# Copying the displaced signs of a binary shift convolution by GpSimd alone, with three sign buffers and transfers by channel tile

## The chip, the cores and the metric

The kernel runs on one core of one Trainium2 chip. The metric is the device time of one execution in microseconds (us). Of the kernel before there are three runs: 2382.28, 2384.86 and 2385.98 us, so the median is 2384.86 us. A separate profiled execution took 2382.86 us, and the span that its trace shows is 2381.1 us.

## The reference

The input `x` has one image of 384 channels and 192 x 192 pixels in float32. Two layers are applied, each as a residual on a group norm over 32 groups of 12 channels (`_gn`).

```
x = x + _L0_conv_ref(_gn(x), ...)   # layer 0: 1x1 conv to q,k,v; 2x2 max pool; 3x3 depthwise conv;
                                    # channel attention, four top-k softmaxes; gelu; repeat 2x2; 1x1 conv
x = x + _L1_conv_ref(_gn(x), weight, bias)
```

Layer 1 is the part that the change touches:

```
def _L1_conv_ref(x, weight, bias):
    K = 7
    xb, wb = sign(x), sign(weight)
    dx = (jnp.arange(C) + K // 2) % K - K // 2
    xp = jnp.pad(xb, ((0, 0), (0, 0), (0, 0), (P, P)))
    idx = jnp.arange(W)[None, :] + dx[:, None] + P
    shifted = jnp.take_along_axis(xp, idx[None, :, None, :], axis=3)
    return jnp.einsum('bchw,oc->bohw', shifted, wb) + bias[None, :, None, None]
```

Each channel's signs are shifted along the row by its own `dx`, one of -3 to 3 (about 55 channels have each value), with zeros moved in at the row's ends, and then a 384 x 384 matrix of signs is applied at every pixel. Because only the sign of the group norm is used, the mean of the group is needed and the variance is not.

## The kernel before

The 384 channels lie as three channel tiles (`CT` = 3) of 128 partitions. The 192 rows are cut into 24 units (`NU`) of 8 rows, so one tile `xt` holds three channel tiles of 1536 float32 values on each partition, 2304 KB in all. The first 2030 us of the span are the statistics of layer 0, its q and k (lines 311 to 366), the softmaxes, and v with the attention. They leave the attention's output in six `chunk` tiles, each of four units. The change leaves their instructions as they are.

The last stage, under `with end:` (line 592), does the rest of both layers for one unit after another. It begins when the group means of layer 1 (`nmean1`, line 587) are known. For each unit there are three steps, whose order is written out by hand:

- `summed(i)` ends layer 0 for the i-th unit of the list `order`. For each of three output channel tiles TensorE runs six matmuls on the chunk into `yps` (L488), and VectorE adds the result to `xt` in two instructions (L497). There are two `yps` buffers. When the last unit of a chunk is done, the chunk's buffer takes an x tile.
- `signed(i)` makes the signs. ScalarE writes them as fp8 into `signs`, in six instructions of 64 partitions (L667): three channel tiles, two halves of partitions. The channels are sorted by shift on the host (`shift_halves`), so that nearly all of a half have one shift, and the half is written displaced by it. In each half, 9 or 10 channels have shift 0 and fill it up. These are written with the wrong displacement, and `centred` brings them back: the rows are copied to `rest`, by small DMAs for channel tiles 0 and 1 (L644) and by GpSimd in 16-bit words for tile 2 (L646), and then GpSimd copies them from `rest` to the right place in `signs` (L655). That copy works byte by byte in tiles 0 and 2, whose place is odd, and in 16-bit words in tile 1.
- `finished(i)` applies the sign matrix: 36 fp8 matmuls into `l1ps` (L687, three buffers of two banks), and six VectorE instructions that add the product and the bias to `xt` in place (L695).

Two sign buffers alternate. The loop runs `summed(i + 2)`, `finished(i)`, `signed(i + 2)`. So the signs of unit i + 2 are written into the buffer that `finished(i)` has just read, while TensorE goes on with `summed(i + 3)` and `finished(i + 1)`.

The data moves in whole units. `stored(i - 2)` is issued on ScalarE's DMA queue from within `signed(i)` (L703). Loads are on SyncE's queue (L171), which also carries the small copies of L644. A load into the buffer of an earlier unit waits on that queue for that unit's store. At the stage's start three units are there (`FIRST`, which are units 19 and 18, and unit 23), and a fourth buffer, `more`, takes a load. The other buffers come free with the chunks.

Of the kernel before, what the change touches and what calls it, by code (L numbers as in the profile page):

```python
# [10 lines left out]
F32 = mybir.dt.float32  # L11
F8 = mybir.dt.float8e4
U16 = mybir.dt.uint16
BF16 = mybir.dt.bfloat16
AF = mybir.ActivationFunctionType
ALU = mybir.AluOpType
# [3 lines left out]
P = 128  # L20
C = 384
CT = C // P
# [8 lines left out]
UR = 8  # L31
NU = H // UR
# [6 lines left out]
PITCH = W + 4  # L39
LEAD = 4  # L40
SLEN = UR * PITCH
HALF = P // 2

STEP = 1584
SAT = [16 + t * STEP + t - SHIFT // 2 for t in range(CT)]
SALL = SAT[-1] + SLEN + PITCH + 9
REST = 32
NREST = [[9, 9], [9, 9], [10, 9]]
ABLK = 512
NAB = NPX // ABLK  # L50
UC = 4
# [8 lines left out]
FIRST = (NU - UC - 1, NU - UC - 2)  # L60
# [17 lines left out]
def shift_halves():  # L78


    dx = lambda c: (c % SHIFT + SHIFT // 2) % SHIFT - SHIFT // 2
    of = {d: [c for c in range(C) if dx(c) == d] for d in range(-(SHIFT // 2), SHIFT // 2 + 1)}
    shift = [[t - SHIFT // 2, t + 1] for t in range(CT)]
    at = np.zeros((P, CT), int)
    for t in range(CT):
        for h, d in enumerate(shift[t]):
            n = NREST[t][h]
            at[h * HALF : (h + 1) * HALF, t] = of[d][:REST] + of[0][:n] + of[d][REST:]
            of[0] = of[0][n:]
    assert sorted(at.flat) == list(range(C))  # L90
    return at, shift


XCH, HSHIFT = shift_halves()


def pair_rows():
# [40 lines left out]
def conv_preact_kernel(ctx: ExitStack, tc: tile.TileContext, a: dict, out: bass.AP):  # L138
    nc = tc.nc
    xv = a["x"].rearrange("u t p n -> u p t n")  # L140
    ov = out.rearrange("u t p n -> u p t n")
# [4 lines left out]
    big = ctx.enter_context(tc.tile_pool(name="big", bufs=NBIG))  # L146
# [5 lines left out]
    parts = {name: small[:, i:j] for name, i, j in SMALL}  # L152
# [7 lines left out]
    nmean1 = const.tile([P, CT], F32, name="nmean1")  # L160
# [6 lines left out]
    def unit(u, pool=big, parts=1):  # L167
        xt = pool.tile([P, CT, UPX], F32, name="xt", tag="big")
        n = CT // parts
        for t in range(0, CT, n):  # L170
            nc.sync.dma_start(xt[:, t : t + n], xv[u][:, t : t + n])  # L171
        return xt
# [36 lines left out]
    kept = {}  # L209
    with tc.tile_pool(name="p1", bufs=1, side="right") as p1, tc.tile_pool(name="p1ps", bufs=2, space=PSUM) as psp:  # L210
# [5 lines left out]
        for i in range(NU):  # L216
            u = NU - 1 - i
            xt = unit(u, parts=CT if u in (0, NU - 1) else 1)
# [13 lines left out]
            else:  # L232
                b, k = divmod(seen, BATCH)
                seen += 1
                for t in range(CT):
                    for j in range(UPX // 512):
                        at = (k * (UPX // 512) + j) * 6
# [14 lines left out]
        more = p1.tile([P, CT, 2], F32, name="more")  # L252
# [26 lines left out]
        shift = p1.tile([NG, 1], F32, name="shift")  # L279
# [59 lines left out]
    with tc.tile_pool(name="p2w", bufs=1, side="right") as wp, tc.tile_pool(  # L339
        name="p2t", bufs=2, side="right"  # L340
    ) as tp, tc.tile_pool(name="p2qkv", bufs=3, space=PSUM) as pqkv, tc.tile_pool(
        name="p2tr", bufs=2, space=PSUM
# [4 lines left out]
        for u in range(NU):  # L347
            xt = kept.pop(u) if u in kept else unit(u)
            lo, hi = rows(u)
            n = hi - lo + 1  # L350
# [149 lines left out]
    with ExitStack() as vs:  # L500
# [39 lines left out]
        for u in range(NU):  # L540
            xt = unit(u)
# [9 lines left out]
            for m in range(CT):  # L551
                parts = []
                for c in range(first // CR, last // CR + 1):
                    r0, r1 = max(first, c * CR), min(last, c * CR + CR - 1)
# [37 lines left out]
    with end:  # L592
        more, sp = opened("p5x1", 1), opened("p5s", 1)
        pyp, psp = opened("p5py", 2, space=PSUM), opened("p5ps", 3, space=PSUM)
        signs = [sp.tile([P, SALL], F8, name=f"signs{i}") for i in range(2)]
        rest = sp.tile([P, CT, SLEN], F8, name="rest")

        def half_rows(sg, t, h):

            at = SAT[t] - HSHIFT[t][h]  # L600
            return sg[h * HALF : (h + 1) * HALF, at : at + SLEN].rearrange("p (r w) -> p r w", w=PITCH)[:, :, :W]


        assert SALL % 4 == LEAD % 4 == PITCH % 4 == 0
        for sg in signs:
            words = sg.bitcast(F32)
            for t in range(CT):
                for h in range(2):
                    at, odd = divmod(SAT[t] - HSHIFT[t][h] - LEAD, 4)
                    assert not odd  # L610
                    lead = words[h * HALF : (h + 1) * HALF, at : at + (UR + 1) * PITCH // 4]
                    nc.gpsimd.memset(lead.rearrange("p (r w) -> p r w", w=PITCH // 4)[:, :, : LEAD // 4], 0.0)
        order = [u for c in reversed(range(NCH)) for u in reversed(range(c * UC, (c + 1) * UC))]
        order = [*FIRST, *(u for u in order if u not in FIRST)]
        left = [UC] * NCH
        free = [more]
        todo = [u for u in order if u not in kept]
        home = {u: big for u in kept} | {FIRST[0]: early}

        def loads():  # L620
            while free and todo:
                u = todo.pop(0)
                home[u] = free.pop(0)
                kept[u] = unit(u, home[u])

        def summed(i):

            u = order[i]
            if i >= len(FIRST):
                for m in range(CT):  # L630
                    projected(pyp.tile([P, PPX], F32, name="yps"), u, m)
            left[u // UC] -= 1
            if not left[u // UC]:
                free.append(big)
                loads()

        def centred(sg, t):

            for h in range(2):
                p = slice(h * HALF + REST, h * HALF + REST + NREST[t][h])  # L640
                at = SAT[t] - HSHIFT[t][h]
                src, to = sg[p, at : at + SLEN], rest[p, t]
                if t < CT - 1:
                    nc.sync.dma_start(to.bitcast(F32), src.bitcast(F32))  # L644
                else:
                    nc.gpsimd.tensor_copy(to.bitcast(U16), src.bitcast(U16))  # L646
            for h in range(2):
                p = slice(h * HALF + REST, h * HALF + REST + NREST[t][h])
                src, to = (
                    v.rearrange("p (r w) -> p r w", w=PITCH)[:, :, :W]  # L650
                    for v in (rest[p, t], sg[p, SAT[t] : SAT[t] + SLEN])
                )
                if SAT[t] % 2 == 0:
                    src, to = src.bitcast(U16), to.bitcast(U16)
                nc.gpsimd.tensor_copy(to, src)  # L655

        def signed(i):


            if i > 2:  # L660
                free.append(home[order[i - 3]])
                loads()
            xt, sg = kept[order[i]], signs[i % 2]
            for m in range(CT):
                for h in range(2):
                    p = slice(h * HALF, (h + 1) * HALF)
                    nc.scalar.activation(  # L667
                        half_rows(sg, m, h),
                        xt[p, m, :].rearrange("p (r w) -> p r w", w=W),
                        AF.Sign,  # L670
                        bias=nmean1[p, m : m + 1],
                        saturate=False,
                    )
                if m == 0 and i > 1:
                    stored(i - 2)
                centred(sg, m)

        def finished(i):

            xt, sg = kept[order[i]], signs[i % 2]  # L680
            for m in range(CT):
                for r0 in range(0, UR, 4):
                    ps = psp.tile([P, 2, 512], F32, name="l1ps")
                    for j in range(2):
                        for t in range(CT):
                            at = SAT[t] + (r0 + 2 * j) * PITCH
                            nc.tensor.matmul(  # L687
                                ps[:, j, : 2 * W],
                                wb[:, t, m * P : (m + 1) * P],
                                sg[:, at : at + 2 * PITCH].rearrange("p (r w) -> p r w", w=PITCH)[:, :, :W],  # L690
                                start=(t == 0),
                                stop=(t == CT - 1),
                            )
                    blk = xt[:, m, r0 * W : (r0 + 4) * W].rearrange("p (j n) -> p j n", j=2)
                    nc.vector.scalar_tensor_tensor(  # L695
                        blk, ps[:, :, : 2 * W], bl1[:, m : m + 1], blk, ALU.add, ALU.add
                    )
                if i >= NU - 2:
                    nc.scalar.dma_start(ov[order[i], :, m], xt[:, m])

        def stored(i):
            u = order[i]
            nc.scalar.dma_start(ov[u], kept.pop(u))  # L703

        with tc.manual_schedule():
            loads()
            for i in range(2):
                summed(i)
                signed(i)
            for i in range(NU):  # L710
                if i + 2 < NU:
                    summed(i + 2)
                finished(i)
                if i + 2 < NU:
                    signed(i + 2)


# [70 lines left out]
```

## Time and profile before

| what | value |
|---|---|
| median of three runs | 2384.86 us |
| span of the profile | 2381.1 us |
| busy, whole span | TensorE 91%, VectorE 77%, ScalarE 37%, GpSimd 10% |
| last stage | from 2030.6 us (the group means) to 2381.1 us |
| moved in the last stage | 21 loads and 24 stores of 2304 KB |

The share of TensorE says little of the last stage. The page's rows of tenths, in 40 slices of 59.5 us, show the last six at TensorE 7, 8, 9, 8, 8 and 7 tenths where all before from the third on are at 9, and GpSimd is at work in these alone. In a group's row the number after the bar is the busy time in us and the mean of one instruction in ns; after the second bar stands how long the engine sat idle just before these instructions, and what it waited for.

### The profile page before, as it was taken

Reading aid. Unit: us, or ns where it says so; the run is one execution under the profiler, and the core shown is the slowest. Engines: PE = TensorE matmul, PEld = TensorE weight load, DVE = VectorE, ACT = ScalarE, POOL = GpSimd, SP = SyncE. Lnnn points to the kernel's source line nnn. Section 1 sums busy time; section 2 is a strip of 40 time slices with the busy share of each in tenths; the row PEclk is TensorE's granted clock in tenths of the full one; section 3 lists DMA queues with packets and bytes.
Section 4 is the critical chain, followed back from the end, with each engine's and each line's share of the span. In section 5 each row is a group of like instructions: output and inputs, shape, how many; then the busy total and the mean of one; then the engine's idle time right before and its main releaser. Section 6 shows DMA issues by size and latency. Waiting matters only on the chain.

```text
span 2381.1 us, 19521 instructions
## 1 busy us (share of the span) xinstructions
PE 2166.2 (91%) x6573; PEld 1032.4 (43%) x6573; DVE 1826.7 (77%) x3113; ACT 878.2 (37%) x1564; POOL 227.5 (10%) x248
## 2 busy tenths in 40 slices
PE   1049999999999999999999999999999999789887
PEld 0024444454444454444444444444444444445444
DVE  4667777777777777777777789986878788678776
ACT  5532223322222332222322232244332323666665
POOL 0000000000000000000000000000000000646676
PEclk7569999999999999999999999999999999899998
DMA  9961111111111211110111022041212122499975
GB/s 398 418 248 40 40 40 46 74 40 40 40 40 40 80 40 40 40 40 0 60 60 40 1 88 101 1 166 73 80 45 115 40 94 90 179 369 364 372 293 209
DMA packets 48948, 272.90 MB, mean 115 GB/s; under 512 B 2896, under 2 KB 5072, under 8 KB 48848
## 3 DMA queue, kind: packets, MB, share of 16 engines
q1 hardware_dynamic: 37392, 211.34, 23.0%
q10 hardware_dynamic: 11456, 60.33, 6.3%
q8 instruction: 51, 0.84, 0.1%
q14 instruction: 49, 0.40, 0.1%
HBM read 213.68 MB, written 56.62 MB: 114 GB/s over the span
## 4 chain that ended last, share of the span: by engine, by line
PE 46%; DVE 33%; DMA 9%; ACT 8%; POOL 2%; issue 2%; SPq 0%; POOLq 0%; DVEq 0%; ACTq 0%
PE qkv L311 33%; DVE dw L334 18%; DVE pooled L318 9%; DMA xt<-in_x_dram 6%; PE l1ps L687 4%; DVE chunk L334 4%; DMA rest<-signs 3%; ACT pooled L325 3%; ACT dw L332 3%; PE gram L366 3%; PE yps L488 2%; PE ops L528 2%; PE tr L362 2%; DVE xt L497 2%; ACT sq L355 2%
## 5 line engine op out<-in xcount | busy, mean ns | idle before, releaser
L311 PE MATMUL qkv<-xt,wq 128*128 128x512 f32 x3888 | 1700.8, 593 | 0.3 <-DVE small L284 0.3
L311 PEld LDWEIGHTS qkv<-xt,wq 128*128 128x128 f32 x3888 | 726.4, 190 | 862.7 <-issue 797.4
L334 DVE SCALAR_TENSOR_TENSOR dw<-pooled,small,dw 128x384 f32<-128x384 f32 (+2 forms) x1152 | 709.3, 616 | 251.3 <-ACT dw L332 226.8
L318 DVE TENSOR_REDUCE pooled<-qkv 128x128 f32<-128x512 f32 x648 | 443.1, 685 | 79.2 <-PE qkv L311 72.9
L334 DVE SCALAR_TENSOR_TENSOR chunk<-pooled,small,chunk 128x384 f32<-128x384 f32 (+3 forms) x696 | 370.4, 546 | 73.5 <-ACT chunk L332 56.0
L336 ACT COPY pooled<-pooled 128x196 f32<-128x196 f32 x207 | 73.7, 356 | 743.2 <-DVE dw L334 520.4
L667 ACT ACTIVATE signs<-xt,nmean 64x1536 fp8e4<-64x1536 f32 x144 | 226.5, 1573 | 108.8 <-POOL signs L655 64.3
L325 ACT ACTIVATE pooled<-pooled,small 128x384 f32<-128x384 f32 x216 | 133.2, 617 | 332.3 <-DVE pooled L318 332.3
L687 PE MATMUL l1ps<-signs,wb 128*128 128x384 fp8e4 x864 | 163.2, 346 | 42.4 <-POOL signs L655 39.5
L655 POOL COPY signs<-rest 9x1536 fp8e4<-9x1536 fp8e4 (+1 forms) x144 | 180.5, 1254 | 133.2 <-DMA rest<-signs 127.0
L695 DVE SCALAR_TENSOR_TENSOR xt<-l1ps,small,xt 128x768 f32<-128x768 f32 x144 | 137.6, 1010 | 52.0 <-issue 23.1
L497 DVE SCALAR_TENSOR_TENSOR xt<-yps,small,xt 128x768 f32<-128x768 f32 x132 | 127.9, 1013 | 30.2 <-PE yps L488 24.3
L488 PE MATMUL yps<-chunk,wpr 128*128 128x384 f32 x396 | 138.4, 495 | 9.1 <-DVE xt L497 9.1
L687 PEld LDWEIGHTS <-wb 128*128 128x128 fp8e4 x864 | 88.1, 102 | 119.8 <-issue 64.3
L292 POOL MEMSET pooled<- 128x196 f32 x9 | 2.4, 267 | 1403.1 <-PE tr L362 1244.8
L355 ACT ACTIVATE sq<-dw 128x384 f32<-128x384 f32 (+2 forms) x144 | 75.3, 523 | 158.2 <-DVE dw L334 158.2
L238 DVE BATCH_NORM_STATS2 stats<-xt 128x6 f32<-128x512 f32 x144 | 87.2, 675 | 59.3 <-DMA xt<-in_x_dram 59.3
L188 PE MATMUL gsps<-sums,small 128*32 128x2 f32 x6 | 0.5, 197 | 127.0 <-DVE sums L259 127.0
L332 ACT ACTIVATE dw<-pooled,small 128x384 f32<-128x384 f32 (+2 forms) x144 | 100.8, 700 | 30.3 <-PE tr L362 28.1
L488 PEld LDWEIGHTS yps<-chunk,wpr 128*128 128x128 f32 x396 | 73.4, 191 | 64.9 <-PE yps L488 15.6
L229 ACT ACTIVATE junk<-xt 128x1536 bf16<-128x1536 f32 x48 | 71.1, 1482 | 52.5 <-DMA xt<-in_x_dram 51.3
L362 PEld LDWEIGHTS tr<-ident,dw 128*128 128x128 f32 (+2 forms) x438 | 52.2, 140 | 70.4 <-DVE dw L334 30.9
(114 smaller groups left out, 676.6 us busy)
## 6 DMA issues: line engine op xcount, KB each, us to landing
xt<-in_x_dram SPq DMA_DIRECT2D x87, 2304.0 KB
out_dram<-xt ACTq DMA_DIRECT2D x22, 2304.0 KB
xt<-in_x_dram SPq DMA_DIRECT2D x6, 768.0 KB
out_dram<-xt ACTq DMA_DIRECT2D x6, 768.0 KB
wq<-in_w_qkvT_dram ACTq DMA_DIRECT2D x1, 1728.0 KB
rest<-signs SPq DMA_DIRECT2D x96, 13.8 KB
wl<-in_w_projG_dram ACTq DMA_DIRECT2D x1, 576.0 KB
wpr<-in_w_projT_dram ACTq DMA_DIRECT2D x1, 576.0 KB
```

The costliest lines, as they stand in the source:

```text
L311: nc.tensor.matmul(ps, wq[:, t, m * P : (m + 1) * P], x4[:, t, r0 : r0 + nr, c0 : c0 + ncol], start=(t == 0), stop=(t == CT - 1),)
L318: nc.vector.tensor_reduce(pl[:, 2 + r0 // 2 : 2 + (r0 + nr) // 2, 1 + c0 // 2 : 1 + (c0 + ncol) // 2], ps.rearrange("p (i a j b) -> p i j ...
L325: nc.scalar.activation(new, new, AF.Identity, bias=bq[:, m : m + 1])
L332: nc.scalar.activation(acc2, src, AF.Identity, bias=bdw[:, m : m + 1], scale=wdw[:, m, 0:1])
L334: nc.vector.scalar_tensor_tensor(acc2, src, wdw[:, m, k : k + 1], acc2, ALU.mult, ALU.add)
L355: nc.scalar.activation(sq[:, : n * WP], acc, AF.Square, accum_out=ssq[:, m, u : u + 1])
L488: nc.tensor.matmul(ps, wpr[:, t, m * P : (m + 1) * P], o[:, t, :], start=(t == 0), stop=(t == CT - 1),)
L497: nc.vector.scalar_tensor_tensor(x5[:, m, r], yb, bpr[:, m : m + 1], x5[:, m, r], ALU.add, ALU.add)
L655: nc.gpsimd.tensor_copy(to, src)
L667: nc.scalar.activation(half_rows(sg, m, h), xt[p, m, :].rearrange("p (r w) -> p r w", w=W), AF.Sign, bias=nmean1[p, m : m + 1], saturate=F ...
L687: nc.tensor.matmul(ps[:, j, : 2 * W], wb[:, t, m * P : (m + 1) * P], sg[:, at : at + 2 * PITCH].rearrange("p (r w) -> p r w", w=PITCH)[:, ...
L695: nc.vector.scalar_tensor_tensor(blk, ps[:, :, : 2 * W], bl1[:, m : m + 1], blk, ALU.add, ALU.add)
```

## The change

The change is to the last stage and to the order of the channels.

- The layout. Of the two halves of a channel tile, the first is now filled up with channels of the second half's shift (9 or 10 of them), and the second with channels of shift 0 (18 or 19). The first half's fillers are then a multiple of four bytes away from their place.
- The copies. `moved` takes the place of `centred`. GpSimd alone copies the fillers of a half to `rest` in 32-bit words (8 rows of 48 words), and then back: in 32-bit words for the first half (392 in a row), and for the second half in bytes (tiles 0 and 2) or 16-bit words (tile 1). The small DMAs are gone. Each half's copies follow that half's ScalarE instruction.
- Three sign buffers take the place of two, and the loop runs `summed(i + 2)`, `signed(i + 2)`, `finished(i)`. The first steps are three `summed`, two `signed`; then `summed(3)`, `signed(2)`, `finished(0)`, `signed(3)`, `finished(1)`, and from there in step.
- Transfers go by channel tile, 768 KB each, and all on SyncE's queue. As soon as a channel tile of a unit is finished it is stored, and the same piece of the tile takes the next unit's load, which waits for that store. On the queue a unit gives: store 0, store 1, load 0, store 2, load 1, load 2. A chunk that comes free takes three more loads.
- The order of the units puts the rest of the chunk of `FIRST` ahead of the others, so that this chunk comes free first.
- The margins between rows are cleared by whole-buffer memsets (five) rather than by twelve small ones.

```diff
-NREST = [[9, 9], [9, 9], [10, 9]]
+NSIGN = 3
...
-        for h, d in enumerate(shift[t]):
-            n = NREST[t][h]
-            at[h * HALF : (h + 1) * HALF, t] = of[d][:REST] + of[0][:n] + of[d][REST:]
-            of[0] = of[0][n:]
+        for h, (d, e) in enumerate(zip(shift[t], (shift[t][1], 0))):
+            n = HALF - len(of[d])
+            at[h * HALF : (h + 1) * HALF, t] = of[d][:REST] + of[e][:n] + of[d][REST:]
+            of[e] = of[e][n:]
+            other[-1].append((e, n))
...
-        signs = [sp.tile([P, SALL], F8, name=f"signs{i}") for i in range(2)]
-        rest = sp.tile([P, CT, SLEN], F8, name="rest")
+        signs = [sp.tile([P, SALL], F8, name=f"signs{i}") for i in range(NSIGN)]
+        rest = [sp.tile([P, SLEN], F8, name=f"rest{i}") for i in range(2)]
+        for ts in (*signs, *rest):
+            nc.gpsimd.memset(ts.bitcast(F32), 0.0)
...
+        ahead = [*FIRST, NU - 1, *(u for u in order if u // UC == FIRST[0] // UC and u not in FIRST)]
+        order = [*ahead, *(u for u in order if u not in ahead)]
...
+        def moved(sg, t, h):
+            d, n = OTHER[t][h]
+            p = slice(h * HALF + REST, h * HALF + REST + n)
+            src, to = SAT[t] - HSHIFT[t][h], SAT[t] - d
+            by = rest[t % 2]
+            nc.gpsimd.tensor_copy(
+                rows_of(by.bitcast(I32), p, 0, PITCH // 4, W // 4),
+                rows_of(sg.bitcast(I32), p, src // 4, PITCH // 4, W // 4),
+            )
+            if d:
+                nc.gpsimd.tensor_copy(sg.bitcast(I32)[p, to // 4 : (to + SLEN) // 4], by.bitcast(I32)[p])
+            elif to % 2 == 0:
+                nc.gpsimd.tensor_copy(
+                    rows_of(sg.bitcast(U16), p, to // 2, PITCH // 2, W // 2),
+                    rows_of(by.bitcast(U16), p, 0, PITCH // 2, W // 2),
                 )
+            else:
+                nc.gpsimd.tensor_copy(rows_of(sg, p, to), rows_of(by, p))
...
-                if m == 0 and i > 1:
-                    stored(i - 2)
-                centred(sg, m)
+                    moved(sg, t, h)
...
+            v = todo.pop(0) if todo else None
+            def load(m):
+                if v is not None:
+                    nc.sync.dma_start(xt[:, m], xv[v][:, m])
...
-                if i >= NU - 2:
-                    nc.scalar.dma_start(ov[order[i], :, m], xt[:, m])
-        def stored(i):
-            u = order[i]
-            nc.scalar.dma_start(ov[u], kept.pop(u))
+                nc.sync.dma_start(ov[u, :, m], xt[:, m])
+                if m:
+                    load(m - 1)
+            load(CT - 1)
...
-            for i in range(2):
+            v = todo.pop(0)
+            kept[v] = unit(v, more, parts=CT)
+            for i in range(3):
                 summed(i)
-                signed(i)
+                if i < 2:
+                    signed(i)
             for i in range(NU):
-                if i + 2 < NU:
+                if i == 0:
+                    summed(3)
+                elif i > 1 and i + 2 < NU:
                     summed(i + 2)
-                finished(i)
                 if i + 2 < NU:
                     signed(i + 2)
+                finished(i)
```

## Prediction

> **What bounds the kernel now.** The change touches only the last stage, so I read that alone, from 2030.6 us, where the chain of waits leaves `nmean` (L587), to 2381.1. I began with the page's groups and the waits of this stretch, to see which wait ends last for each engine.
>
> ```profile
> L667 ACT ACTIVATE signs<-xt,nmean 64x1536 fp8e4<-64x1536 f32 x144 | 226.5, 1573 | 108.8 <-POOL signs L655 64.3
> L687 PE MATMUL l1ps<-signs,wb 128*128 128x384 fp8e4 x864 | 163.2, 346 | 42.4 <-POOL signs L655 39.5
> L655 POOL COPY signs<-rest 9x1536 fp8e4<-9x1536 fp8e4 (+1 forms) x144 | 180.5, 1254 | 133.2 <-DMA rest<-signs 127.0
> ...
> POOL signs L655 <- DMA rest<-signs: 127.0, 39, 23.0
> ...
> PE l1ps L687 <- POOL signs L655: 39.5, 14, 4.5
> ```
>
> TensorE waits for GpSimd's copies, and these wait for the small DMAs. (The longest of those waits, 23.0 us, is GpSimd's before the stage's first signs.) Next, TensorE in order of time, in a stretch without a stall and at the end. Columns: start, length, line, count, idle before.
>
> ```profile
> 2302.05 4.03 PE L488 MATMUL yps<-chunk,wpr 128*128 128x384 f32 x12
> 2306.28 2.17 PE L488 MATMUL yps<-chunk,wpr 128*128 128x384 f32 x6 [0.19 <-DVE xt L497]
> 2308.29 6.24 PE L687 MATMUL l1ps<-signs,wb 128*128 128x384 fp8e4 x36
> 2314.36 4.03 PE L488 MATMUL yps<-chunk,wpr 128*128 128x384 f32 x12
> ...
> 2357.04 8.53 PE L687 MATMUL l1ps<-signs,wb 128*128 128x384 fp8e4 x36 [4.52 <-POOL signs L655]
> 2368.40 7.40 PE L687 MATMUL l1ps<-signs,wb 128*128 128x384 fp8e4 x34 [2.83 <-POOL signs L655]
> ```
>
> From 2302.05 to 2314.36 is one unit without a stall: 12.3 us, of which TensorE idles 0.2. So 12.3 us is TensorE's price for `summed` (6.2) with `finished` (6.1). The last two units, which have no `summed`, take more than 8 us because the signs come late. The chain shows one such stall:
>
> ```profile
> 2190.85 11.56 DMA rest<-signs
> ...
> 2203.32 1.47 POOL signs L655
> ...
> 2211.45 7.62 PE l1ps L687 x34
> ```
>
> A small copy issued in this stretch took 11.6 us. Where the DMA engines are free (2033.9) the same step takes 3.2. The stages show the reason, the DMA share (last but one column):
>
> ```profile
> 2190.00:2200.00 10.00, 9.99 (x49) 5.74 (x48) 9.06 (x11) 7.16 (x6) 0.42 (x1) 1.00 1.01 418
> 2200.00:2210.00 10.00, 3.66 (x11) 1.54 (x10) 4.76 (x5) 6.23 (x4) 7.80 (x8) 0.93 1.02 424
> 2302.20:2314.50 12.30, 12.10 (x56) 6.79 (x55) 11.36 (x13) 9.43 (x7) 9.42 (x10) 1.00 0.50 198
> ```
>
> While loads run, the engines are full at 418 to 424 GB/s and the small copy stands behind megabytes; in the second row TensorE works 3.7 of 10 us.
>
> How much is stall? The first full run of `finished(0)` starts at 2045.4 and the last L695 ends at 2376.9: 331.5 us. In it lie 21 units with `summed` and three without: 21 x 12.3 + 3 x 6.1 = 276.6, and 2 us of VectorE at the end. **52.9 us are stall.** Part is the wait for signs, part the wait for x at the start (VectorE's L497 waited 5.9 us for loads near 2069 and 2097), part TensorE restarting: the row with 34 matmuls above took 7.62 us where 36 take 6.24.
>
> **What the Trainium skill says.** "GPSIMD Engine Reference", section 4.1, says that one-input element work runs at roughly line rate on GpSimd. The trace agrees, per element and not per byte: 1536 bytes take 1468 ns, 768 16-bit words 827 and 784 take 841, so about 0.83 ns an element and 187 ns an instruction. 32-bit copies are not in the trace. "SBUF — State Buffer", section "Who interferes with whom", says that a VectorE instruction with at most one SBUF input does not contend with GpSimd. L497 and L695 read one tensor from PSUM and one from SBUF, and L695 spreads only from 1006 to 1019 ns beside busy GpSimd. "DMA: Bandwidth & Descriptors", section "Issuing engines are not separate DMA queues", says that the queues share the same 16 DMA engines; so the move of the stores to SyncE's queue should by itself cost no bandwidth. Before has loads alone on that queue at 417 GB/s (20 to 100 us), but no mixed traffic on one queue.
>
> **The change part by part.**
>
> *Copies.* Removed: 4 DMAs and 8 GpSimd copies per unit (4 at 1468, 2 at 827, 2 at 841: 9.2 us). Added: 6 copies of 384 words (0.83 x 384 + 187 = 507 ns), 3 of 392 words (514), 2 of 1536 bytes (1468), 1 of 768 (827): 3.04 + 1.54 + 2.94 + 0.83 = 8.4 us, with 0.06 between instructions (the chain's "issue" pieces) 9.1. GpSimd works beside TensorE's 12.3, so this is hidden. The unknown is the 32-bit rate. If a word costs 4 times as much as a byte (bytes moved at the byte copy's rate), the nine copies cost 9 x 1.48 = 13.3 instead of 4.6 and a unit 17.8: GpSimd would be the bound. I take the price per element: 16-bit words cost no more than bytes, and the page's memset of 128x1152 float32 took 1067 ns, 0.93 ns a word. Eighteen partitions where there were nine: I take the same duration, as 10 cost what 9 did. Each second copy waits for the first on the same engine; its own queue alone stands behind it.
>
> *Third buffer and order.* ScalarE needs 6 x 1.573 = 9.4 us a unit and GpSimd 9.1, both under 12.3, and `signed(i + 2)` no longer waits for `finished(i)`. It has two units' time where it had one. So the wait of L687 for signs goes, but for the first units: signs 0 start at 2030.7, ScalarE ends at 2040.1, and GpSimd's last pair (2.0 and gaps) at 2042.2, where before it was 2045.4. Meanwhile TensorE does `summed(2)` and `summed(3)` from 2029.3 to about 2042 (3 x 2.1 each). `finished(0)` is 2042.2 to 2048.3. Signs 1 end on ScalarE at 2049.6 and on GpSimd at 2051.8: a hole of 3.5 us. `finished(1)` ends at 2057.9.
>
> *Sum on TensorE.* From there 20 units of 12.3 to 2303.9, two of 6.1 to 2316.1, VectorE's last 2 us to 2318.1, and the last store's 4.2 us (2376.9 to 2381.1 before): **2322.3**. Checked the other way: stalls 52.9, one `summed` moved ahead 6.2, earlier start 3.2, less the hole 3.5, is 58.8 us; 2381.1 - 58.8 = 2322.3.
>
> *Transfers.* A transfer of 0.786 MB at 418 GB/s takes 1.9 us, so six take 11.3 us a unit, under 12.3. Load 0 waits for store 0 with only store 1 behind it, and load 2 for store 2 with only load 1. The round from one transfer's end to the next one's start I put at up to 2.7 us, from the 3.2 us of a free small copy, which moves almost nothing. That leaves two holes of 0.8 us, so a unit costs the DMA engines 12.9. A chunk's extra load adds 5.7. Is x in time? Store 0 of unit 0 goes at 2045.5; load 2 behind it lands near 2058, and `summed(4)` starts at 2057.9. After `summed(4)`, near 2064, the first freed chunk takes a load; behind load 2 of unit 1 (to about 2067) it ends near 2073. Index 9 of `order` is loaded behind unit 4, three units on: 2073 + 3 x 12.9 = 2112, wanted by `summed(9)` at 2057.9 + 5 x 12.3 = 2119. Index 14: 2073 + 7 x 12.9 + 5.7 = 2169, wanted 2181. Index 19: 2073 + 11 x 12.9 + 11.3 = 2226, wanted 2242. So the loads keep ahead, by little; I add 3 us for what collides. SyncE's queue is in order: behind a load that waits stand only later stores and loads, and while it waits the one or two transfers issued before it run.
>
> *Stores off ScalarE's queue, memsets.* An issue there took 0.38 us beside its arithmetic; nothing. The memsets, 3 x 1239 and 2 x 392 words, come to 4.4 us at the rate above, in place of 1.8, and begin as before near 2010, ahead of the signs at 2030.7: hidden. Everything earlier has the same instructions in the same order.
>
> So the span is 2322.3 + 3 = 2325, and the runs lie 1.8 (the profiled one) to 3.8 (the median) above the span: **2328 us**, 2.4% faster.
>
> **The rivals.**
>
> *DMA sets the pace.* Mixed traffic on one queue may not reach 418 GB/s, or the rounds are longer. For it: the shares of 1.01 above, and 71.7 us that SyncE's loads already wait for stores. Against: units wait for loads only if the sum outruns the lookahead. At 16 us a unit, index 23 lands at 2073 + 14 x 16 + 17 = 2314, wanted at 2292: 22 us later, **2350**.
>
> *GpSimd sets the pace.* At 15 us a unit, between the prices above, 20 units cost 2.7 more each, 54 us: 2328 + 54 = **2382**, no change; at 17.8, 2440. Against: the per-element prices of three kinds of copy and the memset.
>
> *Slower.* If a store and its load never overlap another transfer, six cost 6 x (1.9 + 2.7) = 27.6 us a unit, and 20 units 15 us more each: about **2630**. Against: on the queue two stores go out before the first load waits. Between, a unit at 18.5 us would give about the time of before (2073 + 14 x 18.5 + 17 = 2349, 57 us late).
>
> **How the numbers follow.** TensorE's pace with stalls up to about 12 us: 0.70. The DMA pace, 2340 to 2365: 0.18. GpSimd's pace near the time of before: 0.06. Slower by transfers: 0.03. Something that brings more than 2322 allows (TensorE faster when it never pauses): 0.03. Of GpSimd's 0.06 I put 0.02 each on faster, same and slower. Faster is 0.70 + 0.18 + 0.03 + 0.02 = 0.93; same 0.02; slower 0.02 + 0.03 = 0.05. The range 2318 to 2354 takes the first case whole and most of the second.
>
> **What would show it.** Right: TensorE's units at 12.3 us from about 2058 on, L687 waiting for signs only in the first two, copies of 384 words at 0.5 us, no `rest` DMA, the last unit's matmuls in 6.2 us. The DMA share near 1 until the loads end, then half. Wrong: L497 waiting tens of us for loads (DMA), GpSimd busy without a gap and L667's successors waiting for it (GpSimd), or gaps in the DMA share while loads are still to come (rounds).

## The result, and the profile after

The changed kernel takes **2368.89 us** (median of four runs, 2368.26 to 2373.18), the kernel before 2385.42 beside it (2382.28 to 2386.96): ratio 0.9936, 95% interval 0.9919 to 0.9953. It is faster, as forecast, but by 16.5 us and not by 57, and the time lies above the range of 2318 to 2354.

First the rows of the page and the waits of the last stage (from 2025 us), for the groups that were shown of before. The line numbers have moved: L680 was L687, L655 was L667, L502 was L497, and L647 makes the byte copies that were L655. A line of waits names who waited and for what, then the total in us, the number of waits and the longest.

```profile
L655 ACT ACTIVATE signs<-xt,nmean 64x1536 fp8e4<-64x1536 f32 x144 | 226.5, 1573 | 74.5 <-DVE xt L502 64.9
L680 PE MATMUL l1ps<-signs,wb 128*128 128x384 fp8e4 x864 | 154.7, 335 | 19.1 <-DVE xt L688 15.4
L502 DVE SCALAR_TENSOR_TENSOR xt<-yps,small,xt 128x768 f32<-128x768 f32 x132 | 128.0, 1013 | 38.6 <-DMA xt<-in_x_dram 22.2
```

```profile
DVE xt L502 <- DMA xt<-in_x_dram: 22.2, 15, 2.5
...
PE l1ps L680 <- POOL signs L647: 3.5, 1, 3.5
```

TensorE's wait for signs has gone from 39.5 us to a single 3.5. A new wait stands in its place: VectorE waits 22.2 us, 15 times, for loads of x, and ScalarE and TensorE wait for VectorE. GpSimd's groups, kept apart by shape, show that the copies are not the reason:

```profile
L633 POOL COPY rest<-signs 18x384 int32<-18x384 int32 x48 | 24.3, 507 | 13.4 <-ACT signs L655 12.0
L640 POOL COPY signs<-rest 9x392 int32<-9x392 int32 x48 | 24.3, 505 | 3.0
```

TensorE in order of time: the stage's start, and its last three units.

```profile
2051.67 8.64 PE L680 MATMUL l1ps<-signs,wb 128*128 128x384 fp8e4 x34 [3.47 <-POOL signs L647]
2060.15 4.03 PE L493 MATMUL yps<-chunk,wpr 128*128 128x384 f32 x12
...
2072.45 4.03 PE L493 MATMUL yps<-chunk,wpr 128*128 128x384 f32 x12
...
2323.34 14.92 PE L680 MATMUL l1ps<-signs,wb 128*128 128x384 fp8e4 x90 [1.73 <-DVE xt L688]
```

The hole of 3.5 us is there, the next unit starts at 2060.15 (forecast 2057.9), and 12.3 us later comes the one after it. This pace holds to about 2131, where the waits for x first reach TensorE. TensorE ends at 2338.3, 22 us later than forecast. VectorE ends at 2339.3, and then 27.5 us follow in which only stores run (forecast 4.2). The two make up the miss: 21.2 us at VectorE's end and 23.3 behind it, so a span of 2366.8 where 2322.3 was worked out.

The issues on SyncE's queue, in order of time (start, length with the waits for the next one, line, count), show what the stores do. L673 is a load, L691 a store:

```profile
2137.47 0.34 SPq L673 DMA_DIRECT2D xt<-in_x_dram  x1
2137.92 0.36 SPq L691 DMA_DIRECT2D out_dram<-xt  x1
2139.32 7.27 SPq L673 DMA_DIRECT2D xt<-in_x_dram  x2
2146.70 0.85 SPq L691 DMA_DIRECT2D out_dram<-xt  x2
2153.46 0.34 SPq L673 DMA_DIRECT2D xt<-in_x_dram  x1
...
2315.71 35.73 SPq L691 DMA_DIRECT2D out_dram<-xt  x24
```

From one load 0 (2137.47) to the next (2153.46) is 16.0 us, more than TensorE's 12.3. (The eleven such steps of the stage that have no chunk's loads between take 14.4 to 17.3 us, 15.6 on average.) The store of channel tile 2 (2137.92) waits behind load 0, which waits for store 0. Loads 1 and 2 then span 7.27 us of the queue, since load 2 waits for that store. After the last load at 2315, 24 stores are still to be issued, although TensorE has finished 21 of 24 units and 63 pieces could have gone: the queue is five units late.

The stages of two microseconds in the same unit have, as last two columns, the DMA share and GB/s:

```profile
2143.50:2145.50 2.00, 1.99 (x13) 1.09 (x12) 2.00 (x3) 1.97 (x2) 1.88 (x3) 1.00 1.02 425
2145.50:2147.50 2.00, 2.00 (x13) 1.26 (x12) 2.00 (x3) 1.95 (x3) 1.69 (x4) 1.00 0.60 114
2147.50:2149.50 2.00, 2.00 (x8) 1.14 (x7) 1.49 (x3) 1.27 (x1) 1.35 (x4) 1.00 0.65 138
...
2151.50:2153.50 2.00, 2.00 (x7) 1.11 (x8) 1.75 (x2) 1.96 (x2) 0.35 (x1) 1.00 1.03 430
...
2200.00:2300.00 100.00, 89.90 (x402) 50.16 (x401) 85.49 (x91) 70.32 (x46) 61.41 (x90) 0.98 0.93 314
2340.00:2366.00 26.00, 0.00 (x0) 0.00 (x0) 0.00 (x0) 0.00 (x0) 0.00 (x0) 0.52 0.95 396
```

The engines reach 425 and 430 GB/s when they have work, fall to a quarter or a third of it between, and average 314 over 100 us. That is 31.4 MB in 100 us, while 12.3 us units of 4.72 MB would need 384 GB/s. The share hardly tells: it stays at 0.93. Last, what SyncE's queue waited for:

```profile
SPq L673 <- DMA out_dram<-xt: 217.3, 48, 11.3
```

48 loads waited 217 us for stores; in the kernel before 15 loads waited 71.7 us.

### The profile page after: what moved, and what is told of

It is laid out like the page before. It is cut to its first block, busy times and chain, and to the rows that moved or that the text cites. A ratio compares the mean times of both kernels' runs of the same rounds, so it can differ in the third digit from the quotient of the medians.

```text
span 2366.8 us, 19538 instructions
## 1 busy us (share of the span) xinstructions
PE 2155.2 (91%) x6573; PEld 1029.2 (43%) x6573; DVE 1825.2 (77%) x3113; ACT 878.2 (37%) x1564; POOL 208.5 (9%) x337
## 4 chain that ended last, share of the span: by engine, by line
PE 47%; DVE 33%; ACT 8%; DMA 8%; issue 2%; SPq 0%; POOL 0%; DVEq 0%; ACTq 0%
PE qkv L316 33%; DVE dw L339 18%; DVE pooled L323 9%; DMA xt<-in_x_dram 6%; PE l1ps L680 5%; DVE chunk L339 4%; PE yps L493 3%; ACT pooled L330 3%; ACT dw L337 3%; PE gram L371 3%; DMA out_dram<-xt 2%; PE ops L533 2%; PE tr L367 2%; ACT sq L360 2%; DVE xt L502 1%
## 5 line engine op out<-in xcount | busy, mean ns | idle before, releaser
L655 ACT ACTIVATE signs<-xt,nmean 64x1536 fp8e4<-64x1536 f32 x144 | 226.5, 1573 | 74.5 <-DVE xt L502 64.9
L680 PE MATMUL l1ps<-signs,wb 128*128 128x384 fp8e4 x864 | 154.7, 335 | 19.1 <-DVE xt L688 15.4
L502 DVE SCALAR_TENSOR_TENSOR xt<-yps,small,xt 128x768 f32<-128x768 f32 x132 | 128.0, 1013 | 38.6 <-DMA xt<-in_x_dram 22.2
L688 DVE SCALAR_TENSOR_TENSOR xt<-l1ps,small,xt 128x768 f32<-128x768 f32 x144 | 136.1, 1010 | 8.0 <-ACT signs L655 4.0
L680 PEld LDWEIGHTS <-wb 128*128 128x128 fp8e4 x864 | 85.4, 99 | 89.3 <-issue 33.3
L367 PE MATMUL tr<-ident,dw 128*128 128x128 f32 (+2 forms) x438 | 74.3, 279 | 8.9 <-DVE dw L339 8.1
```

What stands on the lines that cost most here:

```text
L367: nc.tensor.transpose(ps[:L, t * P : (t + 1) * P], dwo[s * CT + t][:, c0 : c0 + L], ident)
L502: nc.vector.scalar_tensor_tensor(x5[:, m, r], yb, bpr[:, m : m + 1], x5[:, m, r], ALU.add, ALU.add)
L655: nc.scalar.activation(rows_of(sg, p, SAT[t] - HSHIFT[t][h]), xt[p, t, :].rearrange("p (r w) -> p r w", w=W), AF.Sign, bias=nmean1[p, t : ...
L680: nc.tensor.matmul(ps[:, j, : 2 * W], wb[:, t, m * P : (m + 1) * P], rows_of(sg, slice(0, P), SAT[t])[:, r0 + 2 * j : r0 + 2 * j + 2], sta ...
L688: nc.vector.scalar_tensor_tensor(blk, ps[:, :, : 2 * W], bl1[:, m : m + 1], blk, ALU.add, ALU.add)
```

## The experiments

**Theory A** (mine after the result): the loads' waits for stores hold the one in-order queue, so later stores, whose data are ready, aren't issued and the DMA engines run dry. **Theory B**: pieces of 768 KB move more slowly than units of 2304 KB. **Theory C**: one queue with loads and stores mixed is slow. After the first four runs A was left. The expectations of runs five to eight use the letter A, or A', for a theory of their own, which each states; the ninth is again about this one. Ratios are against the kernel before. The first four change only transfers of the changed kernel.

**1. The stores on ScalarE's queue.**

```diff
-                nc.sync.dma_start(ov[u, :, m], xt[:, m])
+                nc.scalar.dma_start(ov[u, :, m], xt[:, m])
```

> The changed kernel with one edit: the stores of the channel tiles are issued on ScalarE's queue, the loads stay on SyncE's. A load then still waits for its own store, but no later store stands behind that wait. Theory A (the in-order queue: a load that waits for its store holds back the stores behind it, and the DMA engines run dry for the length of a round trip, some 2 us twice a unit): the engines go back to about 400 GB/s, a unit costs them about 12 us, TensorE's 12.3 us sets the pace and no stores are left over at the end: 2328 to 2338 us. Theory B (pieces of 768 KB are too small to reach the rate that 2304 KB reach): the pieces are the same, so 2360 to 2370 us as in the changed kernel. Theory C (stores and loads mixed on one queue move more slowly whatever their order): two queues as before, so also about 2330; A and C are told apart by the next run.

Measured: 2331.69 us, ratio 0.9783 [0.9768, 0.9798], 37 us below the changed kernel. No store stands behind a load's wait now. The pieces are as small as in the changed kernel, so the loss was not B. Loads and stores still share the 16 engines, but not one queue, so C is left to the next run.

**2. One queue, each load a unit later.** A load is issued behind the store of the next unit's same piece; by then its own store is done.

```diff
-                if m:
-                    load(m - 1)
-            load(CT - 1)
+                if owed:
+                    nc.sync.dma_start(*owed.pop(0))
...
+                owed.extend((xt[:, m], xv[v][:, m]) for m in range(CT))
```

> The changed kernel with one edit: all transfers stay on SyncE's queue in pieces of 768 KB, but a piece's load is issued a whole unit later, behind the next unit's store of the same channel tile (store 0, load 0 of the unit before, store 1, load 1 of the unit before, and so on). The store that a load waits for has then long landed. Loads come a unit later, which must cost some 15 to 20 us once, at units 4 and 5, before the first chunk is free. Theory A: no round trip is left on the queue, over 400 GB/s while there is work, stores done with the last unit: about 2340 to 2350 us. Theory C (one queue with mixed traffic is slow): 104 MB at the 310 GB/s of the changed kernel from 2055 us on take 335 us: 2390 us or more. Theory B: the same as C.

Measured: 2338.04 us, 0.9811 [0.9793, 0.9829], 2 us under what was expected. One of its stages:

```profile
2100.00:2200.00 100.00, 98.22 (x438) 54.87 (x436) 92.49 (x99) 75.51 (x48) 66.35 (x96) 1.00 1.01 416
```

One queue with mixed traffic in 768 KB pieces moves 416 GB/s over 100 us, so B and C fall. It is 6.4 us slower than the first run. The loads come a unit later, and in the trace TensorE loses 9.0 us between 2065 and 2095 to waits behind loads of x, where the first run loses 5.0.

**3. Each load straight behind its store**, the order that comes nearest to the forecast's rival "slower".

```diff
-                if m:
-                    load(m - 1)
-            load(CT - 1)
+                load(m)
```

> The changed kernel with one edit the other way: each load stands straight behind its own store (store 0, load 0, store 1, load 1, store 2, load 2), so three round trips a unit lie open where two were partly covered by one transfer each. Theory A: the changed kernel's 15.5 us a unit on the queue are 11.3 of transfer and two holes of 2.1, so a round trip is 2.1 + 1.9 = 4.0 us; three uncovered ones make 11.3 + 12 = 23.3 us a unit, 7.8 more, and over the 16 units that load this is 125 us: about 2490 us. Theories B and C (a rate, not an order): no change, about 2370 us.

Measured: 2483.44 us (two runs), 1.0419 [1.0395, 1.0444]. The queue shows the round by itself:

```profile
2173.80 0.33 SPq L673 DMA_DIRECT2D xt<-in_x_dram  x1
...
2181.02 0.33 SPq L673 DMA_DIRECT2D xt<-in_x_dram  x1
...
2188.64 0.33 SPq L673 DMA_DIRECT2D xt<-in_x_dram  x1
```

A pair of load and store takes 7.2 and 7.6 us here. Over the whole stage the 43 pairs without a chunk's loads between take 7.0 to 9.6 us, 7.7 on average. The two transfers, at 1.9 each (0.786 MB at 418 GB/s), are 3.8 of it. So a round, from a store's transfer to the start of the load that waits for it, costs **about 3.9 us** beyond the transfers (estimate, from these issues). The changed kernel gives nearly the same: its unit of 15.6 us on average has six transfers, 11.3 us, and two rounds with one transfer beside each, so a round is 1.9 + (15.6 - 11.3) / 2 = 4.0 us, again an estimate. The forecast had 2.7.

Not all of the 3.9 us is a pause. In the third run's trace nothing moves from 2212.4 to 2213.6 us; from there to 2217.2 it is 190 GB/s on average, and 346 in the 2.4 us after that. So with only a load and the next store issued, the engines stand still for about a third of the lost time and run below their full rate for the rest.

**4. Whole units, stores on ScalarE's queue, loads on SyncE's**, as before, with the rest of the change kept.

```diff
-                kept[v] = unit(v, parts=CT)
+                kept[v] = unit(v)
...
-                nc.sync.dma_start(ov[u, :, m], xt[:, m])
-                if m:
-                    load(m - 1)
-            load(CT - 1)
+                if i >= NU - 2:
+                    nc.scalar.dma_start(ov[u, :, m], xt[:, m])
+            if i < NU - 2:
+                nc.scalar.dma_start(ov[u], xt)
             if v is not None:
+                nc.sync.dma_start(xt, xv[v])
```

> The changed kernel with the transfers as before: whole units of 2304 KB, stores on ScalarE's queue, loads on SyncE's into the same buffer; copies, buffers, order of units as changed. Theory A: two queues, nothing held back; but a load starts only when the whole store has landed, so the first units, which have one unit of lookahead, wait some 6 us each: 2335 to 2345 us. Theory B: faster than the run with 768 KB pieces on two queues by 20 us or more. If the gain came from the transfers and not from the copies and buffers, this one would stay near the time of before, 2385 us.

Measured: 2339.31 us, 0.9816 [0.9801, 0.9831]: 7.6 us slower than the first run, which has the small pieces. So the pieces are worth something once nothing is held up; that they are slow was wrong. In the trace of the whole units TensorE waits 6.9 us near 2071 and 1.8 near 2124, where the first run has 5.0 in all, and from its last matmul to the end are 9.0 us, where the first run has 5.5.

**5. The kernel before with the layout and GpSimd's copies alone** (with the memsets that go with them): two buffers, its loop, its order of units and its transfers.

```diff
                     nc.scalar.activation(
...
+                    moved(sg, m, h)
                 if m == 0 and i > 1:
                     stored(i - 2)
-                centred(sg, m)
```

> The kernel before with the copies alone changed: the new layout and GpSimd's word copies in place of the small DMAs; two sign buffers, the old order, whole units, stores on ScalarE's queue and loads on SyncE's. Theory A (the stalls of before were the small DMAs, which stood behind megabytes of x): a unit's signs take ScalarE 9.4 us and GpSimd 2.1 more, and with two buffers 18.5 us are there between one use and the next, so two buffers are enough but for the last unit, which waits some 5.5 us; what is left are the waits for x at the start: 2338 to 2350 us. Rival (one unit's time is too short, the third buffer is the gain): 2370 us or more.

Measured: 2341.95 us, 0.9828 [0.9814, 0.9841]. The copies by themselves bring some 41 us. As the whole change brings 16.5, the rest of it, as written, gives back some 25 us.

**6. The fourth run with the small DMAs and the old layout back**, to see whether a third sign buffer alone hides them. Memory left room for two `rest` tiles only, so tiles 0 and 2 share one.

```diff
...
-                    moved(sg, t, h)
+                centred(sg, t)
...
```

> The run with whole units on two queues and three sign buffers, with the copies alone put back: the old layout, and the small DMAs on SyncE's queue for channel tiles 0 and 1 (two rest tiles in place of three, for want of space). Signs then have two units' time, about 30 us, for 9.4 us of ScalarE, a wait on SyncE's queue behind a load of up to 10, and copies of 10 to 13 us. Theory A' (a third buffer alone hides the small DMAs): 2340 to 2350 us, within 10 of the run without them. Rival (the small DMAs must go): 2365 us or more, with GpSimd waiting for the small DMAs and TensorE for GpSimd.

Measured: 2394.38 us, 1.0050 [1.0035, 1.0065]: slower than the kernel before, and far from what was expected. The waits of the last stage:

```profile
POOL signs L642 <- DMA rest<-signs: 107.6, 25, 15.6
...
PE l1ps L671 <- POOL signs L642: 53.8, 19, 6.6
```

and, on SyncE's queue over the whole run:

```profile
SPq L631 <- POOL signs L642: 161.5, 47, 8.5
```

The small DMAs still stop GpSimd, and TensorE behind it; and now they themselves wait, on the queue that carries the loads, until `rest` is free. That last wait comes from the shared `rest` tile, so the run doesn't say how three sign buffers with three `rest` tiles would have done. That was not tried.

**7. The first run with two sign buffers** and the loop order of before.

```diff
-NSIGN = 3
+NSIGN = 2
...
-            for i in range(3):
+            for i in range(2):
                 summed(i)
-                if i < 2:
-                    signed(i)
+                signed(i)
             for i in range(NU):
-                if i == 0:
-                    summed(3)
-                elif i > 1 and i + 2 < NU:
+                if i + 2 < NU:
                     summed(i + 2)
+                finished(i)
                 if i + 2 < NU:
                     signed(i + 2)
-                finished(i)
```

> The run with the stores on ScalarE's queue (2331.7 us) with two sign buffers and the loop order of before in place of three. Theory A: GpSimd's copies take the signs' latency to 11.6 us, under the 18.5 that two buffers leave, so only the last units lose, 5 to 6 us, and the first some: 2335 to 2342 us. Rival (the third buffer is needed at every unit): 2350 us or more.

Measured: 2340.24 us, 0.9820 [0.9806, 0.9833], so the third buffer with its order is worth 8.5 us against the first run. TensorE near the end:

```profile
2321.66 0.48 PE L680 MATMUL l1ps<-signs,wb 128*128 128x384 fp8e4 x1 [2.25 <-POOL signs L642]
2325.47 7.00 PE L680 MATMUL l1ps<-signs,wb 128*128 128x384 fp8e4 x34 [3.34 <-POOL signs L647]
```

With two buffers a unit hardly stalls either while `summed` covers the signs: TensorE waits for them twice in the middle of the stage, 0.7 and 1.6 us. The last units, which have no `summed`, wait 6.8 us in all. Against the fifth run (old transfers, two buffers) this is the same time: small pieces on two queues bring nothing that these runs can tell there. The third buffer's worth also depends on the transfers: with whole units the fourth run, which has it, is only 2.6 us below the fifth.

**8. The first run, with the first three units' stores on SyncE.** In the first run ScalarE issued unit 0's stores late, between its own instructions: the line of its queue reads

```profile
2052.59 1.84 ACTq L691 DMA_DIRECT2D out_dram<-xt  x3
```

while the changed kernel's queue has the first of them at 2045.5.

```diff
-                nc.scalar.dma_start(ov[u, :, m], xt[:, m])
+                (nc.sync if i < 3 else nc.scalar).dma_start(ov[u, :, m], xt[:, m])
```

> The run with the stores on ScalarE's queue, but those of the first three units on SyncE's as in the changed kernel. In the first run ScalarE had signs to make before it came to the first stores (the first went at 2052.6 us where the changed kernel had it at 2045.5), so the first loads came late and TensorE waited some 6 us between 2067 and 2091. If that is the cause, those waits go: 2325 to 2329 us. If the first loads are late for another cause, no change, 2331 us.

Measured: 2327.76 us, 0.9773 [0.9759, 0.9786]. TensorE keeps 12.3 us a unit from 2060 on in its trace but for one stall of 1.5 us near 2107, where the first run has three between 2065 and 2087, 5.0 us together. The intervals of the two overlap, so the times alone don't show the gain.

**9. One queue, all three stores of a unit ahead of its three loads.**

```diff
                 nc.sync.dma_start(ov[u, :, m], xt[:, m])
-                if m:
-                    load(m - 1)
-            load(CT - 1)
+            for m in range(CT):
+                load(m)
```

> The changed kernel with one edit to the order on SyncE's queue: the unit's three stores first, then its three loads (store 0, 1, 2, load 0, 1, 2). One queue, pieces of 768 KB and everything else as changed. Each load's wait for its own store is now covered by two transfers, 3.8 us, where one covered it, 1.9. Theory A with a round trip of 3.6 to 4.0 us: the holes shrink from about 2 us to 0.2 at most, twice a unit, so a unit costs the engines 11.3 to 11.7 us, under TensorE's 12.3, and no stores are left at the end: 2326 to 2334 us. If the round trip is longer than 5 us, 2 x 1.2 us a unit stay and it is 2340 us or more. If it is one queue as such, or the pieces, no change from 2369.

Measured: **2325.43 us**, 0.9758 [0.9743, 0.9774], the lowest of all and just under what was expected, 43.5 us below the changed kernel by exchanging load 0 and store 2 on the queue. (Its interval overlaps those of the eighth run and, by little, the first.) Its stages, its queue, what the queue waited for, and TensorE at the end:

```profile
2100.00:2200.00 100.00, 98.21 (x437) 54.90 (x436) 92.48 (x99) 76.26 (x49) 66.48 (x97) 1.00 0.98 375
2200.00:2300.00 100.00, 98.41 (x439) 55.14 (x438) 92.06 (x99) 77.03 (x50) 66.94 (x98) 1.00 0.98 382
```

```profile
2095.55 3.97 SPq L673 DMA_DIRECT2D xt<-in_x_dram  x3
2099.61 1.62 SPq L691 DMA_DIRECT2D out_dram<-xt  x3
2107.92 4.08 SPq L673 DMA_DIRECT2D xt<-in_x_dram  x3
```

```profile
SPq L673 <- DMA out_dram<-xt: 156.7, 46, 10.8
SPq L691 <- DVE xt L688: 71.5, 29, 25.9
```

```profile
2299.67 18.05 PE L680 MATMUL l1ps<-signs,wb 128*128 128x384 fp8e4 x108
```

Loads and stores now keep TensorE's pace: 12.4 us from one group of loads to the next, TensorE busy 98%. The loads still wait 156.7 us for stores. What counts is what has been issued ahead of such a wait: load 0 waits for store 0, but stores 1 and 2 run meanwhile, 3.8 us of transfers for a round of about 4. And now stores wait for VectorE: the queue comes to them before their data are there, where it had come five units late. The last three units are 18.05 us without a gap.

## Why the prediction was wrong

- **What bounded the kernel before, and the copies**: right. The signs were TensorE's wait, and the fifth run shows that taking the small DMAs away brings 41 us. A copy of 384 words takes 507 ns, as worked out, one of 392 words 505 (514 was put). Eighteen partitions cost what nine did: 507 ns beside 498 for 384 words, 1467 beside 1468 for 1536 bytes. VectorE's L502 and L688 kept 1013 and 1010 ns beside GpSimd (1013 and 1010 before), as the forecast took from "Who interferes with whom" in the Trainium skill's "SBUF — State Buffer"; the rule there holds only outside VectorE's 2-port perf modes, a condition that the forecast left out and no run here tests.
- **The start**: right within 2.3 us. The hole of 3.5 us is there. `finished(1)` took 8.64 us where 6.1 was put: the clock granted to TensorE in it was 0.65, where it is 0.98 from 2200 to 2300. The forecast had seen TensorE run slower after a pause in the kernel before (7.62 us) and didn't count it here.
- **The third buffer**: right that only the first signs are waited for now. It is worth 8.5 us with these transfers (seventh run), most of it seen at the last units.
- **The transfers: this step failed.** "The round from one transfer's end to the next one's start I put at up to 2.7 us, from the 3.2 us of a free small copy." It is about 3.9 us in the third run and 4.0 in the changed kernel. With one transfer of 1.9 beside each, two rounds of 3.9 leave holes of 4.0 us a unit and not 1.6, so a unit costs the DMA engines 15.3 us and not 12.9, above TensorE's 12.3; 15.6 were measured. The forecast had named the sign, gaps in the DMA share while loads are still to come. The ninth run shows it from the other side: with two transfers beside the round in place of one, nothing else changed, the units take 12.3 and the span is 2323.6, where the sum without the DMA term was 2322.3 and with 3 us for collisions 2325.
- **The queue**: "behind a load that waits stand only later stores and loads" was the right list, and its price was not drawn. The later stores were ready; while they were held back the DMA engines moved only 114 and 138 GB/s in the two stages shown, and the queue fell behind by five units until 2315.
- **The rival of 16 us a unit** came near the pace and the 22 us by which TensorE ends late, and one of its two causes, that "the rounds are longer", is what the runs show. But its 16 was an example and not worked out, so that the numbers agree is in part luck. Its 2350 still added 4.2 us for a last store. With the queue late by five units, some 14 pieces were still to go when VectorE ended (396 GB/s from 2340 to 2366 are 13 of them); at 1.9 us each this is 27 us, and 27.5 were measured. 2350 + 23 = 2373 would have been near 2368.9. The range ended at 2354 because both cases took the end for a single store.
- **GpSimd as the bound**: did not happen (61% busy from 2200 to 2300). **Slower by transfers**: did not happen. The third run is nearest to its order, 2483 us where 27.6 us a unit gave 2630. The rival had a round for each of six transfers, and the third run has one for each pair: three pairs of 7.7 us are 23 us a unit.
- **"Issuing engines are not separate DMA queues"** in the Trainium skill's "DMA: Bandwidth & Descriptors" says that issuing on several engines saves only sequencer time. For bandwidth the runs agree (the second reaches 416 GB/s on one queue). The forecast concluded that moving the stores should by itself cost no bandwidth, and by rate it doesn't. By order it did: on one queue a load's wait holds back the stores behind it, and moving the stores off it, in the first run, is worth 37 us.

**What stays open**: why the engines, after the pause of a round, take some microseconds to come back to their full rate; what the order of the units and the memsets bring, which no run changed alone; and how the small DMAs would do with three `rest` tiles.

## What to carry to other kernels

When a load must wait for a store on the same in-order queue, issue enough ready transfers between the store and the load to fill the round, here about 4 us or two pieces of 768 KB, or give the stores a queue of their own; a DMA share of 0.93 can hide holes, so read GB/s and the queue's own waits. When transfers set the pace, ask at the end how much is still queued: the lag of the queue comes after the last arithmetic. And test a change with several parts one part at a time: here the copies brought 41 us and the rest, with a third buffer worth 8.5 in it, took some 25 back, while with the ninth run's order of issues the same rest brings 16.5 more (2341.95 to 2325.43).

## What was not expected of the hardware

- A store and the load that waits for it on the queue cost about 3.9 to 4.0 us beyond their transfers at full rate (estimates from the third run and the changed kernel). In the third run's trace 1.2 us of this is a pause, and after it the rate is 190 GB/s for 3.6 us. A small copy on free engines, issue to landing, was 3.2 us in the kernel before, and is no upper bound for a round.
- The DMA share stays at 0.60 and 0.65 in stretches of two microseconds in which only 114 and 138 GB/s are moved, where 425 goes with 1.02.
- Loads and stores mixed on one queue, in pieces of 768 KB, reach 425 to 430 GB/s for two microseconds and 416 over 100 us.
- A GpSimd copy is priced by elements and not by bytes: the same 1536 bytes take 507 ns as 384 words of 32 bits and 1467 ns byte by byte.
